# Moving two convolution taps to the start of a period, one accumulator to another bank, and one batch of operand preparation ahead of its use

## The chip, the cores and the metric

The kernel runs on one core of one Trainium2 chip, as one program. The metric is the device time of one execution in microseconds. The time before is a median over 3 runs; the profile is one further execution, recorded by the hardware profiler. The engines are named as the profile names them: PE is TensorE (PEld is its weight load), DVE is VectorE, ACT is ScalarE, POOL is GpSimd, SP is SyncE.

## What is computed

The input is a batch of two images of 128 channels and 64x64 pixels. Four layers follow each other:

```python
x = _L0_conv_ref(...)  # embedding, 2 x (Mamba scan + feed-forward), output projection, residual
x = _L1_conv_ref(...)  # q, k, v by 3x3 convolutions; softmax(q k^T / sqrt(c)) v over 4096 pixels; 1x1 conv; residual
x = _L2_conv_ref(...)  # q, k, v by 1x1 projections; softmax(q k^T) v over 4096 pixels; residual times gamma
x = _L3_conv_ref(...)  # attention over four scales at every pixel
```

The change touches layer 1 (its values) and layer 3. Layer 3, cut to what matters:

```python
for i, scale in enumerate((1, 2, 4, 8)):
    f = conv3x3(mean over scale x scale of x, conv_w[i], conv_b[i])   # scale 1: conv3x3 of x itself
    feats.append(bilinear_resize(f, h, w))
xr = stacked -> (b*h*w, 4, c)
q, k, v = split(xr @ attn_in_w.T + attn_in_b)        # 8 heads of 16 channels
attn = softmax(einsum('nhqd,nhkd->nhqk', q, k) / 4)  # 4 x 4 weights for each pixel and head
res = attn_out(einsum('nhqk,nhkd->nhqd', attn, v)) + xr
normed = layernorm(res)
out = einsum('bchw,oc->bohw', fused 4*c channels of normed, fus_w) + fus_b
```

## The kernel before

All data is fp32, with channels on the 128 partitions. Each layer is a block under a manual schedule: every engine executes its instructions in the order in which the code names them, and semaphores join the engines.

**Layers 1 and 2** are one loop over score units `now`, 128 units for each of four runs: runs 0 and 1 are layer 1 for image 0 and 1, runs 2 and 3 are layer 2. A unit is 128 query pixels by 1024 keys: `score` issues two matmuls (line 709) into a two-bank tile `pq`, and DVE copies it to SBUF with a running maximum (line 714). Later units follow with exponentials on ACT, 128x2048 transposes on DVE (`turn`, line 739), and from unit 14 (`LAG`) on the product with the values (line 759). At unit 13 of each run `values(r)` makes the value tensor. In layer 1 that is a 3x3 convolution in a transformed form: `inputs(r, cc)` makes, in twelve DVE operations of 128x288 elements (lines 589 to 600), six operand planes of a quarter of the image (four in `dlo`, two in a tile `dhi`), `products` multiplies them (line 612, tiles `pa` and `pb`), and `outputs` recombines them (lines 621 to 629). `chunks` walks over the four quarters and prepares the inputs of the next one while PE is at work on this one; the inputs of the first quarter are prepared at the start of `values`.

**Layer 3** works on 16 items (image, strip of 512 pixels). It is a software pipeline: `period(n)` runs for n from -2 to 16, and handles four items at different stages: r = n+2 (convolution at scale 1, features, q and first two k projections), m = n+1 (products of q and k, scores, softmax, v projections), p = n (weights times values, output projection, statistics) and o = n-1 (normalisation, fusion, store). The order inside a period is written by hand. PSUM has four pools here: `mm`, three one-bank tiles for projections, convolution, `po` and so far the fused output `pfus`; `pac`, one bank (tag "acc"), used by the scores `psc` and by the variances `pva` in turn; and `pwp`, one four-bank tile for the weights `pw` and the normalisation factors `prs`. A tile that asks for a bank waits until the last reader of the tile in it is done.

Names used below: conv tap matmul, line 1005, tile `pf`; projections, line 1032, tile `pqkv`; `product`, DVE, line 1049, tile `prod`; `scores`, line 1056; `weights`, line 1091; `weighted`, DVE, line 1098, tile `ov`; sums of `ov` by `add_ov`, line 1102; `soft_exp`, ACT, line 1074; `soft_sum`, DVE, lines 1080 to 1084; `mix_out`, lines 1111 to 1114; `newton`, lines 1133 to 1135; `factors`, line 1142; `normalise`, DVE, line 1149, tile `cen`; `fuse`, lines 1156 and 1161. Once per image change, `means`, `coarse_conv` (line 963, tile `pcs`) and `columns` for the second image are inserted into periods 2 to 5.

Of the kernel before, what the change touches and what calls it, by code (L numbers as in the profile page):

```python
# [6 lines left out]
F32 = mybir.dt.float32  # L7
# [8 lines left out]
P = 128  # L16
CH = 512
# [12 lines left out]
NS = len(SCALES)  # L30
# [37 lines left out]
def tile_conv_seq(ctx: ExitStack, tc, x, consts, vecs, wemb, wlay, wconv, wdt, wqkv, wsmall, wms, out):  # L68
# [478 lines left out]
    with ExitStack() as s, tc.manual_schedule():  # L547
# [29 lines left out]
        def inputs(r, cc):  # L577

            dhi = st["dhi"] = sp.tile([P, 2, 18, 16], F32, name="dhi", tag="d")
            d = [dlo[:, k] for k in range(4)] + [dhi[:, k] for k in range(2)]  # L580
            b = runs[r][1]

            def x1(k):

                return xt[:, b, 16 * cc : 16 * cc + 18, k : k + W - 3 : 4]

            tt, stt = nc.vector.tensor_tensor, nc.vector.scalar_tensor_tensor
            return [
                lambda: stt(d[0], x1(1), -4.0, x1(3), ALU.mult, ALU.add),
                lambda: stt(d[1], x1(2), -4.0, x1(4), ALU.mult, ALU.add),  # L590
                lambda: tt(d[0], d[1], d[0], ALU.subtract),
                lambda: stt(d[1], d[1], 2.0, d[0], ALU.mult, ALU.subtract),
                lambda: tt(d[2], x1(3), x1(1), ALU.subtract),
                lambda: tt(d[3], x1(4), x1(2), ALU.subtract),
                lambda: stt(d[2], d[2], -2.0, d[3], ALU.mult, ALU.add),
                lambda: stt(d[3], d[3], 2.0, d[2], ALU.mult, ALU.subtract),
                lambda: stt(d[4], x1(2), -5.0, x1(4), ALU.mult, ALU.add),
                lambda: stt(d[4], x1(0), 4.0, d[4], ALU.mult, ALU.add),
                lambda: stt(d[5], x1(3), -5.0, x1(5), ALU.mult, ALU.add),
                lambda: stt(d[5], x1(1), 4.0, d[5], ALU.mult, ALU.add),  # L600
            ]
# [58 lines left out]
        def values(r):  # L660
            vt = st["vt"] = sp.tile([P, N // P, C], F32, name="vt", tag="vt")
            vs = {}

            def turned(cc):
                for i in range(2):
                    pt = psa.tile([P, 4, P], F32, name="pvt", tag="acc")
                    for a in range(4):
                        at = (4 * i + a) * P
                        nc.tensor.transpose(pt[:, a, :], vs[cc][:, at : at + P], ident)
                    at = (2 * cc + i) * 4  # L670
                    nc.scalar.copy(vt[:, at : at + 4, :], pt)

            def to(cc):
                if cc > 1:
                    turned(cc - 2)
                vs[cc] = sp.tile([P, 4 * QG], F32, name="vs", tag="tr", bufs=2)
                return vs[cc]

            if not runs[r][0]:
                for f in inputs(r, 0):  # L680
                    f()
            chunks(r, 2, to)
            turned(NCC - 2)
            turned(NCC - 1)
# [126 lines left out]
        for now in range(NALL + LAG + 10):  # L811
            r, u = divmod(now, NU)
            w = now % 8
            if now < NALL:
                if u == 0:
                    if r == 2:
                        wm = wbig.tile([P, NS, 9, C], F32, name="wm", tag="wbig")
                        nc.sync.dma_start(wm, wms)
                    keys(r)
                    if runs[r][0]:  # L820
                        query(r, 0)

                r4, cc = divmod((now + 16) // 32, NCC)
                v = (now + 16) % 32
                if now >= 16 and r4 < B:
                    if v == 0:
                        ahead = inputs(r4, cc)
                    if v < 6:
                        for f in ahead[2 * v : 2 * v + 2]:
                            f()  # L830
                    if v == 14:
                        queries(r4, cc)
                        if r4 and cc == 0:
                            load(1, HI)
                score(r, u)
                if runs[r][0]:
                    if w == 2 and u // 8 + 1 < NU // 8:
                        query(r, u // 8 + 1)
                elif u == 1:
                    load(2, LO), load(2, HI)  # L840
                elif u == LAG:
                    load(0, LO), load(0, HI)
                    if r == 0:
                        load(1, LO)
            if w == 7:
                at(lambda r, u: finish_mm(r, u // 8), LAG + 9)
            at(product, LAG)
            if w == 7:
                at(lambda r, u: finish(r, u // 8), LAG + 9)
            if w in (3, 7):  # L850
                at(lambda r, u: exponentials(r, u // 4), 3)
            if w in (1, 5):
                at(lambda r, u: turn(r, u // 4, 0), 5)
            if w in (3, 7):
                at(lambda r, u: turn(r, u // 4, 1), 7)
            if w == 2:
                at(lambda r, u: diagonals(r, u // 8), 10)
            if w == 3:
                at(lambda r, u: spread(r, u // 8), 11)
            if w == 5:  # L860
                at(lambda r, u: divide(r, u // 8), LAG + 7)
            if now < NALL and u == LAG - 1:
                values(r)


    with ExitStack() as s, tc.manual_schedule():
# [130 lines left out]

        def conv(i, taps):
            b, c = items[i]
            if taps[0] == 0:  # L1000
                st[i]["pf"] = mmt("pf")
            for tap in taps:
                dy, dx = divmod(tap, 3)
                rhs = xt[:, b, c * RPC + dy : (c + 1) * RPC + dy, dx : dx + W]
                nc.tensor.matmul(st[i]["pf"], lhsT=wm[:, 0, tap, :], rhs=rhs, start=(tap == 0), stop=(tap == 8))  # L1005
# [145 lines left out]
        def fuse(i, sis):  # L1151
            w = st[i]
            if sis[0] == 0:
                w["pfus"] = mmt("pfus")
            for si in sis:
                nc.tensor.matmul(w["pfus"], lhsT=wfus[:, si, :], rhs=w["cen"][:, si, :], start=(si == 0), stop=(si == NS - 1))
            if sis[-1] < NS - 1:
                return
            b, c = items[i]
            ot = sp.tile([P, CH], F32, name="ot", tag="ot")  # L1160
            nc.scalar.activation(ot, w["pfus"], AF.Identity, bias=bfus)
            nc.sync.dma_start(out[b, :, c * RPC : (c + 1) * RPC, :].rearrange("c h w -> c (h w)"), ot)
            w.clear()

        def period(n, extra):
            o, p, m, r = n - 1, n, n + 1, n + 2

            def do(i, f, *a):
                if has(i):
                    f(i, *a)  # L1170

            def more(k):
                for f, a in extra.get((n, k), ()):
                    f(*a)


            do(r, features)
            do(m, project, 2, 0)
            for ti in range(NS):
                do(m, product, ti)  # L1180
                if ti == 0:
                    do(o, normalise)
                do(p, weights, ti)
                if ti + 2 < NS:
                    do(m, project, 1, ti + 2)
                if ti > 0:
                    do(m, scores, ti - 1)
                do(p, weighted, ti)
                if ti == 1 and has(p):
                    add_ov(nc.gpsimd, p, 0, 1)  # L1190
                if ti < 2:
                    do(o, fuse, (2 * ti, 2 * ti + 1))
                else:
                    do(r, conv, (2 * ti - 4, 2 * ti - 3))
                more(ti)
            do(m, scores, NS - 1)

            if has(p):
                add_ov(nc.vector, p, 2, 3)
                add_ov(nc.vector, p, 0, 2)  # L1200
            do(m, soft_max)
            do(r, conv, (4, 5, 6, 7, 8))
            do(r, conv_out)
            for si in range(1, NS):
                do(m, project, 2, si)
            do(m, soft_exp)
            do(m, soft_sum)
            more(4)
            for si in range(NS):
                do(p, mix_out, si)  # L1210
            more(5)

            do(p, variance)
            for si in range(NS):
                if si == 2:
                    do(p, newton)
                do(r, project, 0, si)
            do(r, project, 1, 0)
            do(p, factors)
            do(r, project, 1, 1)  # L1220
            more(6)
# [97 lines left out]
```

## Time and profile before

| | |
|---|---|
| time, median of 3 | 5120.4 us (5120.3 to 5123.17) |
| span of the profiled run | 5118.0 us |
| PE busy | 4685.8 us (92%) |
| DVE busy | 4091.4 us (80%) |
| ACT busy / POOL busy | 2366.8 us (46%) / 2312.5 us (45%) |
| mean granted PE clock | 0.947 of full speed |

Layer 0 fills about the first 42% of the span; layers 1 and 2 run from about 2160 us to 4295 us; layer 3 runs from about 4295 us to the end. A matmul of 128x512 fp32 stands as two records; back to back they start 0.43 us apart, so one such matmul takes 0.86 us of PE. "Idle before" in square brackets is the time that the engine stood still ahead of a row, with the instruction that released it.

### The profile page before, as it was taken

To read this page: it belongs to the slowest core of one execution; us is meant where nothing else is said; L and a number is where in the kernel's file an instruction comes from. 1 tells how busy PE (TensorE), PEld (TensorE's weight loads), DVE (VectorE), ACT (ScalarE), POOL (GpSimd) and SP (SyncE) were. 2 spreads that over 40 slices of the span, in tenths; PEclk is the share of its full clock that TensorE was granted. 3 is DMA by queue.
4 is the path that set the end of the run, shared out by engine and by line. 5 is a ranking of instruction groups with operands and counts; after the bars stand their busy time and mean duration, and the time that the engine had idled before them with its cause. 6 is when DMAs were issued, how large, how long until landed. Compare 5 with 4: busy or idle time off the path is not lost.

```text
span 5118.0 us, 48991 instructions
## 1 busy us (share of the span) xinstructions
PE 4685.8 (92%) x14797; PEld 2250.5 (44%) x14797; DVE 4091.4 (80%) x4416; ACT 2366.8 (46%) x3221; POOL 2312.5 (45%) x1948
## 2 busy tenths in 40 slices
PE   5898899899888998789999999999999998989997
PEld 1222222222222222356666666666666665333332
DVE  5999999999999999588888887667766775757665
ACT  4677777777777777422322222333333332223332
POOL 2777777766777777313332233333333333323221
PEclk8889998998999989899999999999999999999998
DMA  5332323333222333124443244444444442000000
GB/s 151 72 69 69 69 69 71 71 71 69 67 67 67 69 72 72 38 56 104 100 105 86 71 103 105 118 98 111 112 100 98 111 112 62 5 5 7 5 7 9
DMA packets 237017, 373.86 MB, mean 73 GB/s; under 512 B 88001, under 2 KB 88401, under 8 KB 228433
## 3 DMA queue, kind: packets, MB, share of 16 engines
q1 hardware_dynamic: 187600, 303.55, 25.0%
q10 hardware_dynamic: 49152, 67.17, 5.5%
q8 instruction: 118, 1.93, 0.2%
q14 instruction: 147, 1.20, 0.1%
HBM read 92.18 MB, written 9.83 MB: 20 GB/s over the span
## 4 chain that ended last, share of the span: by engine, by line
PE 47%; POOL 19%; DVE 13%; issue 10%; DMA 4%; ACT 3%; SPq 2%; ACTq 0%; DVEq 0%; POOLq 0%
POOL h L387 15%; PE po L759 13%; PE pq L709 13%; DVE tr L739 3%; PE pf L1005 3%; DMA pt<-tr 2%; PE py L399 2%; SPq L750 2%; PE pqkv L1032 1%; PE pu L288 1%; DVE prod L1049 1%; DVE h L384 1%; PE psc L1056 1%; PE pw L1091 1%; POOL dtu L347 1%
## 5 line engine op out<-in xcount | busy, mean ns | idle before, releaser
L746 POOL COPY pt<-tr 32x512 f32<-32x512 f32 x1024 | 652.3, 637 | 1499.3 <-DVE tr L739 766.6
L384 DVE TENSOR_TENSOR_SCAN h<-da,carry,h 128x512 f32<-128x512 f32 x1024 | 1240.7, 1265 | 60.6 <-ACT da L373 30.6
L387 POOL TENSOR_TENSOR h<-h,cb 128x2048 f32<-128x2048 f32 x256 | 1161.2, 4536 | 20.8 <-POOL carry L386 0.2
L709 PE MATMUL pq<-k,q 128*128 128x512 f32 x2048 | 963.9, 594 | 8.5 <-DVE sc L714 6.2
L759 PE MATMUL po<-pt,vt 128*128 128x256 f32 x4096 | 967.3, 379 | 2.4 <-DMA pt<-tr 2.4
L724 ACT ACTIVATE sc<-sc,nm 128x2048 f32<-128x2048 f32 x256 | 510.6, 1995 | 925.4 <-DVE nm L720 670.8
L714 DVE TENSOR_SCALAR_CACHE_REDUCE sc<-pq 128x1024 f32<-128x1024 f32 x512 | 624.8, 1222 | 362.1 <-PE pq L709 340.5
L759 PEld LDWEIGHTS po<-pt,vt 128*128 128x128 f32 x4096 | 779.1, 190 | 295.2 <-issue 211.4
L373 ACT ACTIVATE da<-dtb,am 128x512 f32<-128x512 f32 x1024 | 681.6, 684 | 223.8 <-DVE h L384 212.5
L739 DVE STREAM_TRANSPOSE tr<-sc 128x2048 f32<-128x2048 f32 x256 | 591.7, 2311 | 68.1 <-DMA pt<-tr 61.2
L366 DVE TENSOR_TENSOR h<-bb,pdu 128x2048 f32<-128x2048 f32 x256 | 581.3, 2271 | 77.3 <-PE py L399 29.4
L399 PE MATMUL py<-h,sel 128*32 128x512 f32 x2048 | 511.1, 643 | 1.6 <-POOL h L387 1.6
L709 PEld LDWEIGHTS pq<-k,q 128*128 128x128 f32 x2048 | 383.6, 190 | 286.6 <-issue 247.7
L360 PE MATMUL pdu<-dtu,fsel 128*128 128x512 f32 x512 | 327.3, 725 | 102.5 <-DVE h L366 102.4
L399 PEld LDWEIGHTS py<-h,sel 128*32 128x32 f32 x2048 | 115.3, 118 | 416.3 <-issue 409.4
L288 PE MATMUL pu<-xn,wu 128*128 128x512 f32 x512 | 245.3, 612 | 3.8 <-ACT xn L278 2.0
L360 PEld LDWEIGHTS pdu<-dtu,fsel 128*128 128x128 f32 x512 | 96.3, 215 | 309.7 <-DVE h L366 187.7
L386 POOL COPY carry<-h 128x4 f32<-128x4 f32 x256 | 47.5, 186 | 388.9 <-DVE h L384 388.9
L1032 PE MATMUL pqkv<-f,ws 128*128 128x512 f32 x384 | 189.9, 620 | 11.5 <-DVE prod L1049 9.9
L1098 DVE TENSOR_TENSOR ov<-v,pw 128x2048 f32<-128x2048 f32 x64 | 146.0, 2282 | 50.6 <-PE pw L1091 50.3
L1102 POOL TENSOR_TENSOR ov<-ov 128x2048 f32<-128x2048 f32 x16 | 72.6, 4540 | 240.8 <-DVE ov L1098 240.8
L1016 POOL TENSOR_SCALAR f<-lo 128x256 f32<-128x256 f32 x32 | 27.6, 863 | 315.1 <-PE po L1111 260.5
(241 smaller groups left out, 5387.1 us busy)
## 6 DMA issues: line engine op xcount, KB each, us to landing
pt<-tr SPq DMA_DIRECT2D x2048, 64.0 KB, 2.0
dtb<-dt SPq DMA_DIRECT2D x1024, 64.0 KB, 2.0
pt<-tr ACTq DMA_DIRECT2D x1024, 64.0 KB, 2.2
bb<-dr SPq DMA_DIRECT2D x128, 256.0 KB, 4.7
cb<-dr SPq DMA_DIRECT2D x128, 256.0 KB, 7.7
uw<-ufold SPq DMA_DIRECT2D x14, 576.0 KB, 3.9
xt<-in_x SPq DMA_DIRECT2D x16, 256.0 KB, 5.1
xr<-in_x SPq DMA_DIRECT2D x16, 256.0 KB, 2.9
```

The costliest lines, as they stand in the source:

```text
L360: nc.tensor.matmul(pdu, lhsT=four(s_ % 4), rhs=st[i]["dtu"][:, s_ // 4, :], start=True, stop=True)
L366: nc.vector.tensor_tensor(h, st[i]["bc", 0], pdu.unsqueeze(1).to_broadcast([P, 4, CH]), ALU.mult)
L373: nc.scalar.activation(da, st[i]["dtb", s_], AF.Exp, scale=am[items[i][1]][:, j, gg, m : m + 1])
L384: nc.vector.tensor_tensor_scan(h[:, m, :], da, h[:, m, :], carries[b, l][:, j, gg, m : m + 1], ALU.mult, ALU.add)
L387: nc.gpsimd.tensor_tensor(h, h, st[i]["bc", 1], ALU.mult)
L399: nc.tensor.matmul(py[r : r + 32, :], lhsT=sel, rhs=st[i]["h", s_ + k][:, m, :], start=(m == 0), stop=(m == 3), tile_position=(0, r),)
L709: nc.tensor.matmul(pq[:, i, :], lhsT=st["q", r, grp][:, it * P : (it + 1) * P], rhs=st["k"][:, at : at + CH], start=True, stop=True)
L714: nc.vector.tensor_scalar(dst, pq, 1.0, None, ALU.mult, ALU.max, accum_out=st["mx"][:, c2 : c2 + 1])
L724: nc.scalar.activation(sc, sc, AF.Exp, bias=nm, scale=scale, accum_out=sm[:, hh : hh + 1])
L739: nc.vector.transpose(tr, st.pop(("sc", r, blk, hh)).rearrange("p (t r f) -> p r t f", r=NB, f=32))
L746: nc.gpsimd.tensor_copy(dst, src)
L759: nc.tensor.matmul(st["po", r, grp], lhsT=st["vt"][:, jt, :], rhs=rhs, start=(jt == 0), stop=(jt == N // P - 1))
```

## The change

Three things are changed.

1. In `values`, the twelve `inputs` of the first quarter are no longer made at the start of `values` (unit 13), but two at a time in units 6 to 11, behind the score copy of each unit.
2. In layer 3, the fused output `pfus` takes the one-bank pool `pac` instead of a tile of `mm`, and its four matmuls all stand at step 0 of the period, where they had been split into two at step 0 and two at step 1.
3. In layer 3, the first two taps of item r's convolution are issued at the start of the period, where item m's first v projection had been; the next taps stand at steps 1, 2 and 3, and one tap remains behind the scores. The v projection joins the other three behind the convolution.

The purpose is to give PE work where it waits for DVE at the start of the period and at its second step, and to take DVE work off the start of `values`. The matmuls, vector operations and bytes are the same in number as before.

```diff
@@ values
-            if not runs[r][0]:
-                for f in inputs(r, 0):
-                    f()
             chunks(r, 2, to)
@@ main loop of layers 1 and 2
                 elif u == 1:
                     load(2, LO), load(2, HI)
+                    first = inputs(r, 0)
+                elif 6 <= u < 12:
+                    for f in first[2 * u - 12 : 2 * u - 10]:
+                        f()
@@ fuse
-                w["pfus"] = mmt("pfus")
+                w["pfus"] = pac.tile([P, CH], F32, name="pfus", tag="acc")
@@ period
             do(r, features)
-            do(m, project, 2, 0)
+            do(r, conv, (0, 1))
...
-                if ti < 2:
-                    do(o, fuse, (2 * ti, 2 * ti + 1))
-                else:
-                    do(r, conv, (2 * ti - 4, 2 * ti - 3))
+                if ti == 0:
+                    do(o, fuse, range(NS))
+                do(r, conv, ((), (2, 3), (4, 5), (6, 7))[ti])
                 more(ti)
             do(m, scores, NS - 1)
...
-            do(r, conv, (4, 5, 6, 7, 8))
+            do(r, conv, (8,))
             do(r, conv_out)
-            for si in range(1, NS):
+            for si in range(NS):
                 do(m, project, 2, si)
```

More of the change, by code (lines that the diff above doesn't have):

```diff
@@ L999, in conv @@
             b, c = items[i]
+            if not taps:
+                return
             if taps[0] == 0:
```

## The prediction

> **What bounds the kernel now.** I read the page first: PE is busy 92% and DVE 80%, and the chain of waits puts 47% of the span on PE and 13% on DVE. That is a mean over four layers, so I went to the two places that the diff touches, with the timeline of PE, then of DVE and ACT, over one ordinary period of layer 3 and over both calls of `values`.
>
> One ordinary period of layer 3, from `weights` to `weights`, PE alone. The columns are start, busy time, engine, line; the bracket is idle time ahead of the row:
>
> ```profile
> 4717.63 1.14 PE L1091 MATMUL pw<-at,spread 32*128 32x512 f32 x8 [1.89 <-DVE cen L1149]
> 4718.70 1.13 PE L1032 MATMUL pqkv<-f,ws 128*128 128x512 f32 x2
> 4719.66 1.88 PE L1156 MATMUL pfus<-cen,wfus 128*128 128x512 f32 x4
> 4721.48 1.14 PE L1091 MATMUL pw<-at,spread 32*128 32x512 f32 x8
> 4723.44 1.13 PE L1032 MATMUL pqkv<-f,ws 128*128 128x512 f32 x2 [0.83 <-DVE prod L1049]
> 4724.50 1.07 PE L1056 MATMUL psc<-prod,kc 128*32 128x512 f32 x8
> 4725.50 1.98 PE L1156 MATMUL pfus<-cen,wfus 128*128 128x512 f32 x4
> ...
> 4736.37 4.56 PE L1005 MATMUL pf<-xt,wm 128*128 128x512 f32 x10
> 4740.77 2.74 PE L1032 MATMUL pqkv<-f,ws 128*128 128x512 f32 x6
> 4743.34 1.02 PE L1111 MATMUL po<-f,kc 128*128 128x512 f32 x2
> ...
> 4761.79 1.14 PE L1091 MATMUL pw<-at,spread 32*128 32x512 f32 x8 [1.89 <-DVE cen L1149]
> ```
>
> The period is 4761.79 - 4717.63 = 44.16 us, and PE stands still visibly in two places: 1.89 us, until `normalise` has freed the four-bank tile, and 0.83 us, until `product` 1 has freed the bank that the last k projection takes. Everything else is PE work. The same two waits stand in nearly every period from 1 to 14.
>
> What DVE does there:
>
> ```profile
> 4721.05 2.34 DVE L1049 SCALAR_TENSOR_TENSOR prod<-pqkv,vec,q 128x2048 f32<-128x2048 f32 x1
> 4723.31 2.27 DVE L1098 TENSOR_TENSOR ov<-v,pw 128x2048 f32<-128x2048 f32 x1
> 4725.50 2.34 DVE L1049 SCALAR_TENSOR_TENSOR prod<-pqkv,vec,q 128x2048 f32<-128x2048 f32 x1
> 4728.62 2.29 DVE L1098 TENSOR_TENSOR ov<-v,pw 128x2048 f32<-128x2048 f32 x1 [0.78 <-PE pw L1091]
> ```
>
> Products and weighted values alternate, 2.3 us each, almost without a gap: DVE is close behind PE here.
>
> In `values` of run 1, PE and then DVE:
>
> ```profile
> 2813.93 1.89 PE L759 MATMUL po<-pt,vt 128*128 128x256 f32 x8
> 2821.37 7.89 PE L612 MATMUL pa<-uw 128*128 128x256 f32 x24 [5.54 <-DVE uw L591]
> 2831.68 5.34 PE L612 MATMUL pa<-uw 128*128 128x256 f32 x24
> ```
> ```profile
> 2792.59 1.23 DVE L714 TENSOR_SCALAR_CACHE_REDUCE sc<-pq 128x1024 f32<-128x1024 f32 x1 [1.38 <-PE pq L709]
> 2814.13 1.23 DVE L714 TENSOR_SCALAR_CACHE_REDUCE sc<-pq 128x1024 f32<-128x1024 f32 x1 [1.80 <-PE pq L709]
> 2818.42 1.01 DVE L589 SCALAR_TENSOR_TENSOR uw<-xt 128x288 f32<-128x288 f32 x1
> 2826.65 0.67 DVE L589 SCALAR_TENSOR_TENSOR uw<-xt 128x288 f32<-128x288 f32 x1
> ```
>
> PE waits 5.54 us for the first inputs and then runs its first 24 records in 7.89 us instead of 5.34. The first set of inputs occupies DVE from 2818.42 to 2826.65, 8.2 us. From there to the end of `values` DVE has no gap above 0.3 us: `values` is bound by DVE.
>
> [...] a `pf` that lives from the start of the period to its end leaves two `mm` banks; this is why `pfus` must move. The trace shows no bank but the waits for them (0.83 us above). [...] after 1.89 us a `weights` group takes 1.14 us, after 6.48 us idle (4668.16) a `factors` group takes 2.09 instead of 1.14. [...] an input operation takes 1.08 us beside POOL's copies of transposed blocks and 0.67 without.
>
> **Layer 3, one period.** I lay out the new order from `weights` 0 as time 0, with group times from the rows above (start to start: `weights` 1.07, projection 0.96, scores 1.0, two taps 1.91, fusion matmul 0.86).
> - Start: two taps (1.71 us) replace one projection (0.86). They stand in the 1.89 us wait, which shrinks to 1.03; time 0 does not move, since `cen` sets it through q, `prod`, `prs` on DVE, none of it changed. 0.86 us of PE work is hidden.
> - Step 0: projection k2 at 1.07, four fusion matmuls 2.03 to 5.5, so `weights` 1 at 5.55 instead of 3.85. The k3 projection comes at 6.6; `product` 1 ends at 5.76 (4723.39 - 4717.63), so the 0.83 us wait is gone.
> - New wait 1: `scores` 0 at 7.65 needs the bank that `pfus` holds. Its eviction (0.69 us) is next in ACT's queue and ends at 6.4. No stall; queued behind it on PE are the taps.
> - New wait 2: `weights` 1 comes later, so `weighted` 1 starts at 6.75 instead of 5.68. DVE then stands at 11.3 after `product` 2; `weights` 2 ends at 11.65, `weighted` 2 11.8 to 14.05, `weights` 3 at 14.5 finds it done; DVE ends the sums of `ov` at 23.2 instead of 22.4. PE reaches `po` at 23.9 instead of 25.71, and the half that needs `ov` at 24.8: 1.6 us to spare.
> - ACT: four v evictions end at 24.9; `soft_exp` waits for DVE until 25.4 and ends at 26.0, as the first `po` becomes readable (25.8). At most 0.2 us.
>
> From time 0 to `po` the period so gains 25.71 - 23.9 = 1.8 us, and the rest is unchanged: 42.4 us instead of 44.16.
>
> **Other periods.** Ordinary in this sense are 1, 3, 4 and 6 to 13, 11 periods: 19.7 us. In 3 and 4 a `coarse_conv` at step 1 finds all three banks taken and waits for `product` 2, until about 11.4 with PE there at 10.6; in its place stood 0.87 and 0.78 us of waiting for the eviction, so it is even. In period 2 (`means`) and 5 (`columns`) DVE is the bound behind `soft_sum`, which comes 1.05 us earlier (`soft_exp` ends at 26.0 against 27.1): 1.05 us gained in 2; in 5 the following start has no wait to hide taps in (`weights` at 4673.47 shows none, and PE is at half speed after 6.48 us idle), which costs 1.6 us: net -0.5. Period 0 is bound by DVE in its steps, the taps fill waits of 1.26 and 0.40 us: about +2. Period -1: -0.2. Drain: in 14 there is no convolution left, DVE's later `weighted` costs 0.4; in 15 two more fusion matmuls stand ahead of `weights` 1, for which DVE already waits: 1.8 lost. Sum 19.7 + 1.05 - 0.5 + 2 - 0.2 - 0.4 - 1.8 = 19.9 us. The unknown is DVE's shift: if the 0.8 us on DVE reaches PE the period gains 1.0, if the hidden small waits of PE go too, 2.1: 11 to 24 us.
>
> **Values.** Run 1: PE is busy without a gap in units 6 to 13, DVE has idle time there of 1.38 + 0.25 + 1.33 + 0.24 + 0.72 + 0.25 + 1.80 + 0.24 = 6.2 us. Twelve operations (8.2 us at the price beside POOL, 7.4 at that without) fill it, some 1.5 us spill over. PE is not held up: the score of unit 13 at 2812.22 needs the copy of unit 11, done by 2810.8 even so. PE starts `pa` at 2815.9 at once, and DVE's second set starts at 2820.1 instead of 2826.65: 6.5 us. Behind the two inputs on DVE wait the copies and transposes of the unit; their users come several units later. Run 0: no products exist yet, DVE is the bound already in units 6 to 13, with idle time of about 1 us (0.24 + 0.25 + 0.28 + 0.24), so the 6.53 us PE wait at the start of `values` moves rather than disappears: 1 us. Ends: 4 (idle time only half usable) and 9.5. I take 7.5.
>
> Total 19.9 + 7.5 = 27.4 us: 5093.
>
> **Rivals.**
> - DVE takes over in layer 3: the 1.07 us that `weighted` 1 loses is passed on to `po` or to the next start. For it: DVE is busy 31 of 44 us and its operations stand end to end in the steps. Against: 1.6 us of slack at `po`, idle of 6.35 us ahead of `newton`. Layer 3 then gains about 0.86 x 12 = 10: 5120 - 10 - 7.5 = 5103.
> - The values' inputs gain nothing (they only move DVE work): 5120 - 20 = 5100. For it: run 0. Against: the 6.2 us of idle DVE in run 1.
> - The shared bank becomes the new wait: variances, fused output and scores now run in series through one bank. If the eviction came 3 us late, as behind a blocked ACT, PE would lose 1.8 us net in 12 periods, more than the two waits bring: layer 3 loses 2 us or more beyond its gain, and with values' inputs delaying scores the time would be 5130. Against: ACT is idle 11.05 us ahead of that eviction now.
>
> **Chances.** The forecast 0.62, first rival 0.17, second 0.09, more gain than forecast (hidden waits) 0.07, slower or equal 0.05. The range takes the forecast with the ends of its terms and the first two rivals: 5085 to 5104. Faster by over 0.2% (under 5110) 0.93, same 0.04, slower 0.03.
>
> **What would show it.** Right: periods of about 42.4 us between evictions of `pfus`; the wait for `cen` near 1.0 and that for `prod` gone; no wait of `psc` for the eviction; `pa` of run 1 without wait and 5.3 us long; in run 0 the scores of units 6 to 13 stretched by some 7 us. Wrong: PE waiting for `ov` at `po`, or for the bank at `psc`, or scores of run 1 waiting for DVE in units 8 to 13.

## The result, and the profile after

| | before | after |
|---|---|---|
| time, median of 4 runs each | 5121.65 us (5120.3 to 5123.17) | 5102.76 us (5101.34 to 5104.57) |
| ratio | | 0.9963, 95% interval 0.9946 to 0.998 |
| PE busy in the profiled run | 4685.8 us | 4686.2 us |
| DVE busy in the profiled run | 4091.4 us | 4094.2 us |

The changed kernel is faster by 18.9 us; 27.4 were forecast. Five more runs on another occasion gave 5102.3 us, ratio 0.9963 again (0.9949 to 0.9976). The busy times are as before: what went is waiting. The two executions that were profiled took 5118.0 and 5102.8 us, a difference of 15.2 us; whatever is read from the two traces has to add up to that and not to 18.9.

One ordinary period of layer 3 after the change, the timeline of PE from `weights` to `weights` (columns as before: start, busy time, engine, line; idle time in brackets; line numbers are 3 higher than before):

```profile
4755.46 1.14 PE L1094 MATMUL pw<-at,spread 32*128 32x512 f32 x8 [1.03 <-DVE cen L1152]
4756.53 1.12 PE L1035 MATMUL pqkv<-f,ws 128*128 128x512 f32 x2
4757.50 3.60 PE L1159 MATMUL pfus<-cen,wfus 128*128 128x512 f32 x8
4761.02 1.14 PE L1094 MATMUL pw<-at,spread 32*128 32x512 f32 x8
4762.10 1.13 PE L1035 MATMUL pqkv<-f,ws 128*128 128x512 f32 x2
4763.15 1.06 PE L1059 MATMUL psc<-prod,kc 128*32 128x512 f32 x8
4764.15 1.98 PE L1008 MATMUL pf<-xt,wm 128*128 128x512 f32 x4
...
4775.02 1.13 PE L1008 MATMUL pf<-xt,wm 128*128 128x512 f32 x2
4775.98 3.60 PE L1035 MATMUL pqkv<-f,ws 128*128 128x512 f32 x8
4779.42 1.02 PE L1114 MATMUL po<-f,kc 128*128 128x512 f32 x2
...
4797.87 1.14 PE L1094 MATMUL pw<-at,spread 32*128 32x512 f32 x8 [1.03 <-DVE cen L1152]
```

The period is 4797.87 - 4755.46 = 42.41 us. The wait for `cen` is 1.03 us, the wait for `product` 1 is gone, `po` comes 23.96 us behind `weights` and does not wait for `ov`, and the scores do not wait for the bank.

DVE in the same period:

```profile
4758.88 2.34 DVE L1052 SCALAR_TENSOR_TENSOR prod<-pqkv,vec,q 128x2048 f32<-128x2048 f32 x1
4762.23 2.29 DVE L1101 TENSOR_TENSOR ov<-v,pw 128x2048 f32<-128x2048 f32 x1 [1.01 <-PE pw L1094]
4764.44 2.35 DVE L1052 SCALAR_TENSOR_TENSOR prod<-pqkv,vec,q 128x2048 f32<-128x2048 f32 x1
4767.27 2.29 DVE L1101 TENSOR_TENSOR ov<-v,pw 128x2048 f32<-128x2048 f32 x1 [0.49 <-PE pw L1094]
```

The new wait on DVE is there, 1.01 us ahead of `weighted` 1, and nobody on PE waits for it.

`values` of run 1, PE and then DVE:

```profile
2809.22 1.89 PE L756 MATMUL po<-pt,vt 128*128 128x256 f32 x8
2812.09 0.71 PE L767 MATMUL pr<-dg,kc 128*128 128x128 f32 x4 [0.98 <-DVE dg L761]
2819.53 5.34 PE L612 MATMUL pa<-uw 128*128 128x256 f32 x24
2827.30 5.34 PE L612 MATMUL pa<-uw 128*128 128x256 f32 x24
```
```profile
2793.74 0.68 DVE L589 SCALAR_TENSOR_TENSOR uw<-xt 128x288 f32<-128x288 f32 x1
2794.34 1.12 DVE L590 SCALAR_TENSOR_TENSOR uw<-xt 128x288 f32<-128x288 f32 x1
2823.04 1.04 DVE L589 SCALAR_TENSOR_TENSOR uw<-xt 128x288 f32<-128x288 f32 x1
2824.01 1.11 DVE L590 SCALAR_TENSOR_TENSOR uw<-xt 128x288 f32<-128x288 f32 x1
```

The 5.54 us of waiting ahead of `pa` are gone and `pa` takes 5.34 us. A new wait of 0.98 us stands ahead of `pr`, whose operand `dg` is now queued behind two input operations on DVE.

To see where time went between such places, I followed a mark that comes once per eight score units, the `pr` matmuls of layers 1 and 2, through both traces. The table says how much later (+) or earlier (-) the changed kernel is than the kernel before at each mark, in us; below this is called its lateness:

```
group of run 0, before / behind its values    +7.34 / +0.92   (+0.59 at the end of layer 0)
all further groups of run 0                   +0.93 to +0.96
run 1, before / behind its values             +2.62, +3.76 / -2.26
all further groups of run 1                   -2.22 to -2.26
run 2, before / behind its values             -2.25 / -0.83
run 3, before / behind its values             +0.34 / +2.84, then constant
first coarse convolution of layer 3           +0.92
end                                           -15.2
```

Between starts of runs and their values the difference stands still to 0.05 us. Run 1's values gain 2.62 + 2.26 = 4.9 us. The jumps of +1.7 (start of run 1), +1.4, +1.2 and +2.5 us, and one of -1.9 us between the end of run 3 and layer 3, stand at places that the change does not touch. Together they are +4.9 us: in these two traces they take back all that run 1's values gain.

### The profile page after: what moved, and what is told of

It is laid out like the page before. It is cut to its first block, busy times and chain, and to the rows that moved or that the text cites. A ratio compares the mean times of both kernels' runs of the same rounds, so it can differ in the third digit from the quotient of the medians.

```text
span 5102.8 us, 48990 instructions
## 1 busy us (share of the span) xinstructions
PE 4686.2 (92%) x14797; PEld 2249.2 (44%) x14797; DVE 4094.2 (80%) x4416; ACT 2367.7 (46%) x3221; POOL 2317.8 (45%) x1948
## 4 chain that ended last, share of the span: by engine, by line
PE 46%; POOL 21%; DVE 13%; issue 11%; DMA 4%; ACT 3%; SPq 3%; DVEq 0%; ACTq 0%; POOLq 0%
POOL h L387 17%; PE po L756 13%; PE pq L706 13%; DVE tr L736 3%; DMA pt<-tr 2%; SPq L747 2%; PE pf L1008 2%; PE py L399 2%; PE pqkv L1035 2%; PE pw L1094 1%; POOL dtu L347 1%; POOL z L410 1%; PE pfus L1159 1%; PE pu L288 1%; PE psc L1059 1%
## 5 line engine op out<-in xcount | busy, mean ns | idle before, releaser
L261 PE MATMUL pr<-rs,kc 2*128 2x512 f32 (+1 forms) x128 | 90.2, 834 | 77.3 <-POOL rs L257 71.1
```

## Experiments

Five questions: what each part is worth alone, whether the jumps belong to the change, which edit in layer 3 does it, what start and drain cost, and whether a better order exists. Times are medians, ratios are against the kernel before on the same chip. The experiments ran on three chips, so those of different groups are best compared by what each gains on the kernel before.

**Inputs alone.** Part 1 of the diff on the kernel before.

> Only the first inputs of the values are made ahead; layer 3 is as before. My theory: run 1 gains 4 to 5 us at its values, run 0 nothing, since DVE is the bound there already; then 5117, with up to 3 us more or less from untouched places where PE's clock falls in gaps of about 3 us. Rival (the inputs only move DVE work): 5121.

5115.75 us against 5120.18, ratio 0.9992 (0.9984 to 1.0001). In the marks, run 0 loses 0.1 to 0.3 us at its values (+0.14 here, +0.33 and +0.31 in the two traces of the changed kernel), run 1 gains 4.85. This is the size expected, 4.4 us by the medians, but its interval just touches no change.

**Layer 3 alone.** Parts 2 and 3.

> Only layer 3 is changed (fusion in one block in the other bank, two taps at the start); values as before. My theory: periods of 42.4 us, layer 3 shorter by 15 to 18 us: 5104, give or take 3. Rival (the two parts only pay together): 5110 or more.

5101.63 us, ratio 0.9966 (0.9954 to 0.9977); ordinary periods 42.40 us. Layer 3 is nearly the whole gain. 4.4 + 18.6 is 23.0, while the whole kernel gains 19 on both occasions: see the last experiment.

**The fusion block alone.**

```diff
-                if ti < 2:
-                    do(o, fuse, (2 * ti, 2 * ti + 1))
-                else:
+                if ti == 0:
+                    do(o, fuse, range(NS))      # pfus in pac
+                if ti > 1:
                     do(r, conv, (2 * ti - 4, 2 * ti - 3))
```

> Only the fused output is moved to the scores' bank with its four matmuls at step 0; the taps stay at steps 2 and 3 and behind the scores, the v projection at the start. My theory: the wait for the k bank (0.83 us) goes, but PE has nothing at step 1 to cover the weighted value that comes 1 us later, so waits of some 0.4 us before weights 2 and 0.6 us before weights 3 take its place: period 44.0 to 44.4, time 5121 to 5123. Rival (the fusion block is what gains): period 43.3, time 5111.

5120.48 us, ratio 1.0 (0.9991 to 1.0008). The timeline of PE over one period of it (44 us), the rows of `weights`:

```profile
4724.20 1.14 PE L1091 MATMUL pw<-at,spread 32*128 32x512 f32 x8
4727.75 1.14 PE L1091 MATMUL pw<-at,spread 32*128 32x512 f32 x8 [0.36 <-DVE ov L1098]
4732.21 1.14 PE L1091 MATMUL pw<-at,spread 32*128 32x512 f32 x8 [0.41 <-DVE ov L1098]
4762.61 1.14 PE L1091 MATMUL pw<-at,spread 32*128 32x512 f32 x8 [1.89 <-DVE cen L1149]
```

The wait of 0.83 us is traded for two of 0.36 and 0.41 us: most ordinary periods are 43.97 us instead of 44.16, two of the eight from 6 to 13 are 45.62. What is left of this gain goes in the drain, the last periods: from `weights` of period 14 to the start of the last fusion it takes 84.1 us, where the kernel before takes 79.4. So the block in itself brings nothing; it needs PE work at step 1, and the loss in the drain is its own.

**A later start, nothing else.** In the kernel before, the first of the twelve input operations at the very start of layer 1 is made three times.

```diff
-        for f in inputs(0, 0):
+        head = inputs(0, 0)
+        for f in 2 * head[:1] + head:
             f()
```

> The kernel before, with the first input operation of layer 1 made three times instead of once, so that all of layers 1 to 3 starts 1.3 us later; nothing else differs. My theory (PE's clock falls or not in the 3 us gaps at the starts of runs and in their values[...]): the lateness against before does not stay at 1.3 us, it jumps by 1 to 3 us, up or down, at the keys and values of runs 1, 2 and 3, and is constant between. Rival (the jumps of the changed kernel come from its own changes): 1.3 us throughout, up to the end.

The one execution took 5121.37 us. The added operations did not do what they were meant to do. PE's first products of layer 1 wait for a DMA and not for these operations, and are not held up by the added ones. The kernel before, then this one:

```profile
2155.59 7.98 PE L612 MATMUL pa<-uw 128*128 128x256 f32 x24 [3.77 <-DMA uw<-ufold]
```
```profile
2157.03 8.05 PE L612 MATMUL pa<-uw 128*128 128x256 f32 x24 [3.63 <-DMA uw<-ufold]
```

PE starts 1.44 us later, but at the end of layer 0, ahead of the added operations, it was already 1.6 us late: this lateness is a difference between two executions of the same instructions. What the run still shows is how it goes on: +0.73 in the rest of run 0, +0.72 in run 1, then -0.97 at the start of run 2, +0.43 behind its values, +1.48 from run 3 on. Places that no edit touches moved by -1.7, +1.4 and +1.05 us, and the times between them by nothing. The two traces of the changed kernel itself say the same: the second is 0.8 us earlier than the first all through runs 0 to 2, and 3.3 us earlier from run 3's values on. So jumps of this kind need no change of the kernel. What they are shows in run 3's values, where PE waits equally long in both kernels. Before the change, then after it:

```profile
3851.75 1.09 PE L669 MATMUL pvt<-kc,vs 128*128 128x128 f32 x8 [3.16 <-ACT vs L561]
```
```profile
3852.09 1.97 PE L669 MATMUL pvt<-kc,vs 128*128 128x128 f32 x8 [3.16 <-ACT vs L561]
```

The same eight transposes behind the same wait of 3.16 us take 1.09 us in one trace and 1.97 in the other. The clock granted to PE from 3851 to 3853 us was full in the first (1.00) and half in the second (0.50). In the second trace of the changed kernel they take 1.09 us again. The jump at the start of run 1 is of the same kind: behind a wait of 2.32 us in both traces a `pb` group takes 2.86 us before and 4.39 after, and the granted clock stays at 1.00 in the first (2763.4 to 2766.2 us) and falls to 0.50 in the second (2766.0 to 2768.0 us). The same wait has either outcome, even in two executions of one kernel; what decides between them is not seen in the traces.

**Without taps at the start.** The changed kernel, with the v projection back at the start and the taps one step later.

```diff
-            do(r, conv, (0, 1))
+            do(m, project, 2, 0)
-                do(r, conv, ((), (2, 3), (4, 5), (6, 7))[ti])
+                do(r, conv, ((), (0, 1), (2, 3), (4, 5))[ti])
-            do(r, conv, (8,))
+            do(r, conv, (6, 7, 8))
```

> The changed kernel, but with the v projection at the start of the period as before, and the taps at steps 1, 2 and 3 with three left behind the scores. My theory (the block of fusions removes the k wait if taps cover step 1; the taps at the start are worth 0.86 us a period by themselves): period 43.3, wait for cen 1.89, time about 11 us above the changed kernel. Rival (the taps at the start are what removes both waits): period 44.0 as with the fusion block alone, 20 us above.

5123.19 us, ratio 1.0002 (0.9993 to 1.001): 21 us above the changed kernel, the rival's number, but not for the rival's reason. Its ordinary periods are 43.26 us, as I expected, or 44.91 us, in the order of two long ones to one short one. A short one and a long one, PE from `weights` 0 to `weights` 1:

```profile
4804.11 1.14 PE L1094 MATMUL pw<-at,spread 32*128 32x512 f32 x8 [1.89 <-DVE cen L1152]
4805.18 1.12 PE L1035 MATMUL pqkv<-f,ws 128*128 128x512 f32 x2
4806.14 3.60 PE L1159 MATMUL pfus<-cen,wfus 128*128 128x512 f32 x8
4809.67 1.14 PE L1094 MATMUL pw<-at,spread 32*128 32x512 f32 x8
...
4847.37 1.23 PE L1094 MATMUL pw<-at,spread 32*128 32x512 f32 x8 [1.89 <-DVE cen L1152]
4848.53 2.08 PE L1035 MATMUL pqkv<-f,ws 128*128 128x512 f32 x2
4850.40 4.25 PE L1159 MATMUL pfus<-cen,wfus 128*128 128x512 f32 x8
4854.58 1.14 PE L1094 MATMUL pw<-at,spread 32*128 32x512 f32 x8
```

`weights` 0 to `weights` 1 takes 5.56 us in the first and 7.21 in the second; the projection takes 2.08 us instead of 1.12. The wait of 1.89 us ahead of both is the same. The granted clock is 0.78 on the mean from 4847.2 to 4855.0 us in the long one and 1.00 from 4803.9 to 4808.0 us in the short one. The kernel before had this too, in two of its ordinary periods (44.99 and 44.97 us instead of 44.16); the prediction took no notice of them.

**The wait filled with useless work.** As the last, with one matmul more per period that nobody reads (periods 1 to 13).

```diff
             do(m, project, 2, 0)
+            if has(o) and has(r):
+                wrm = pac.tile([P, CH], F32, name="wrm", tag="acc")
+                nc.tensor.matmul(wrm, lhsT=ident, rhs=kc[:, :CH], start=True, stop=True)
```

> As the kernel without taps at the start (periods of 43.26 and 44.91 us), with one useless 128x512 matmul of 0.86 us in the wait for cen, into the scores' bank, read by nobody. My theory (the 1.89 us wait costs more than itself where PE's clock falls behind it; a wait of 1.03 us does not let it fall): all ordinary periods 43.3, although PE does 0.86 us more each; time about 5111 to 5113, some 10 us below the kernel without taps at the start. Rival (the long periods come from DVE or from banks): 43.26 and 44.91 as without the matmul, 5121 to 5123.

5109.48 us, ratio 0.9979 (0.9971 to 0.9988). PE at one of its periods:

```profile
4837.21 1.02 PE L1184 MATMUL wrm<-kc 128*128 128x512 f32 x2
4839.27 1.14 PE L1094 MATMUL pw<-at,spread 32*128 32x512 f32 x8 [1.03 <-DVE cen L1152]
4840.34 1.12 PE L1035 MATMUL pqkv<-f,ws 128*128 128x512 f32 x2
```

Every period from 6 to 12 is 43.26 or 43.27 us; no long one is left. The next is 44.91 us again: it ends behind the start of period 14, which has no such matmul. Against the kernel before on its own chip this one gains 9.9 us, where the kernel without the added matmul loses 1.5: one matmul per period without a reader makes the kernel some 11 us faster. So the wait of 1.89 us cost more than its length, and the taps at the start are worth their 0.86 us and the clock.

**Taps and the v projection in the wait.**

```diff
+                if ti == 0:
+                    do(m, project, 2, 0)
                 do(p, weights, ti)
...
-            for si in range(NS):
+            for si in range(1, NS):
                 do(m, project, 2, si)
```

> The changed kernel, with the first v projection behind the two taps but still ahead of weights 0, so that both stand in the wait for cen. My theory (the wait of 1.03 us takes another 0.86, DVE still has time to spare at po): period 41.6, 10 us below the changed kernel. Rival (DVE becomes the bound at po): period 42.0 to 42.4 with a wait of po for ov.

5096.15 us, ratio 0.9948 (0.9935 to 0.9962). Ordinary periods are 41.55 us, with 0.17 us of waiting for `cen` and none at `po`. It is 6 us below the changed kernel and not 10: its drain, from `weights` of period 14 to the start of the last fusion, takes 85.8 us against 83.9 there, and the periods 2 and 5, with `means` and `columns` in them, are no shorter than there.

**Start and drain in another order.** As the last, but periods without an item o or r keep the old order, with taps at steps 1 to 3; `pfus` is in `mm` again in periods 14 to 16, where no `pf` exists.

```diff
+            full = has(o) and has(r)
+            if full:
                 do(r, conv, (0, 1))
+            else:
+                do(m, project, 2, 0)
...
+                if not full and ti < 2:
+                    do(o, fuse, (2 * ti, 2 * ti + 1))
```

> As the one with taps and v in the wait, but periods -2 to 0 and 14 to 16, where item o or item r does not exist, have the v projection at the start, fusions in two halves in a bank of mm, and taps at steps 1 to 3. My theory (the start and the drain lost what I had not counted: the k3 projection waiting for product 1 in periods -1 and 0 since pf holds one of three banks, and four fusion matmuls ahead of weights 1 in the drain): 4 to 6 us below the one with taps and v. Rival [...]: within 2 us of it.

5085.71 us, ratio 0.9933 (0.9919 to 0.9946): 10.4 us below the last one, more than expected, and the best of the orders tried without useless work. From the first coarse convolution to `weights` of period 1 it takes 103.7 us instead of 107.6, and 80.0 us instead of 85.8 in the drain.

**PE kept busy in layer 2.** As the last, with six useless matmuls (2.6 us) ahead of the third chunk of keys and values in runs 2 and 3.

> As the kernel with its ends repaired, with six useless matmuls (2.6 us) in the keys and in the values of runs 2 and 3, where PE stands still some 3 us for ACT; read by nobody. My theory (the clock falls in these gaps or not [...], the jumps of 1 to 3 us at these places): no half-speed rows behind the gaps, the lateness against before no longer grows at keys and values of runs 2 and 3, 2 to 4 us below the one with its ends repaired. Rival (the useless matmuls stand in the way of what waits for them): no gain, or up to 4 us lost.

5084.46 us, ratio 0.993 (0.9914 to 0.9947), 1.3 us below the last one but on another chip; against their own kernels before the two gain 34.9 and 36.0 us, so nothing is shown of a gain. In the one trace the lateness falls by 1.7 us at the start of run 2 and of run 3 each, where the changed kernel had risen by 1.2 us at run 3, it no longer rises at either run's values, and the transposes of run 3's values take 1.09 us behind a wait of 0.60 us. That is what the theory expects, but one trace does not show it: without useless matmuls the kernel with the later start also fell by 1.7 us at run 2, and the one without taps at the start does not rise at either run's values.

**The changed kernel again.**

> The changed kernel once more, since each part alone summed to more (4.4 and 18.6 us by medians) than the whole gained in its first four runs (18.9). If the parts add up: 5097. If the whole loses in its own way[...]: 5102 to 5103 again.

5102.3 us over 5 runs, so the parts do not add up, by some 4 us, which the interval of the inputs alone would just allow. The marks of this trace have jumps of +1.7, +1.4 and +1.2 us at starts and values of runs 1 to 3. Such jumps come without any edit of those places, as the two experiments with a later start and with the fusion block alone show too; in the traces before and after the change the granted clock differs at each of the three (1.00 and 0.64, 1.00 and 0.54, 0.69 and 0.55). But the first of them, at the start of run 1, stands in all eight traces of kernels with the inputs made ahead, measured against the one trace of the kernel before, and in one of the three others, the fusion block alone. That would make some of the missing time a cost of making the inputs ahead; with one trace each, whether it does stays open.

## Why the forecast was right in direction and too large

The time of 5102.76 us lies inside the range of 5085 to 5104, but by 1.2 us only, and at the number that the first rival named (5103), though that rival's mechanism is absent from the rows. The mechanism forecast for the ordinary period is in the rows; that the errors in the other terms left the total just inside the range is luck.

Held, with what was measured: the ordinary period (42.4 forecast, 42.41); the wait for `cen` (1.03) and that for `product` 1 (gone); no wait of the scores for the shared bank, no wait at `po`; `means` (1.05 forecast, 0.94 gained); coarse convolutions even (0.80 us of waiting in each of the two, where 0.87 and 0.78 had been); the stretched scores of run 0 (some 7 us forecast, 6.75). `columns` held in the first trace of the changed kernel (-0.5 forecast, -0.56), but in its second trace the same period is 1.6 us shorter. The first rival (DVE takes over) and the third (the shared bank) fell by the same rows. The second (the inputs gain nothing) held for run 0 and failed for run 1.

Four terms of the sum were mis-sized.

1. Start, periods -1 and 0: +1.8 us forecast, -2.0 measured (from the first coarse convolution to `weights` of period 1, 105.7 us before and 107.7 after). The waits in period 0 that the taps were to fill did go, but one new wait came in each of the two periods. I counted the `mm` banks for an ordinary period, where the fusion block covers the time until `product` 1, but not for periods without an item o. `pf` holds one bank from the start on, so the last k projection has to wait there, and in period 0 the clock fell behind the wait (0.55 granted from 4379.8 to 4381.9 us, where period -1 has 1.00 from 4351.9 to 4353.1). The timeline of PE after the change:

```profile
4351.92 1.13 PE L1035 MATMUL pqkv<-f,ws 128*128 128x512 f32 x2 [1.13 <-DVE prod L1052]
4379.88 1.97 PE L1035 MATMUL pqkv<-f,ws 128*128 128x512 f32 x2 [1.12 <-DVE prod L1052]
```

2. Drain: -2.2 us forecast, -4.5 measured to the start of the last fusion (79.4 us before, 83.9 after), -3.2 to its end, since that fusion takes 6.41 us before and 5.18 after. The cause was right, and the fusion block alone shows the same loss; its price was taken at full clock. In period 15, at a granted clock of 0.74 (5053.3 to 5058.3 us), the block takes

```profile
5053.32 4.94 PE L1159 MATMUL pfus<-cen,wfus 128*128 128x512 f32 x8
5058.20 1.14 PE L1094 MATMUL pw<-at,spread 32*128 32x512 f32 x8
```

where four matmuls take 3.60 us otherwise (at 1.00 from 4755.4 to 4759.0 us), and DVE waits for `weights` 1 behind it; `weights` 3 of the same period takes 2.09 us instead of 1.14 (0.50 granted from 5065.3 to 5067.5 us). The order with repaired ends, which undoes 1 and 2 on top of the taps and the v projection, returned 3.9 and 5.8 us there.

3. Values: 7.5 us forecast, about 4.5 measured (run 1 4.9 of 6.5, run 0 -0.3 of 1). In run 1 the work did go into DVE's idle time, and DVE's second set of inputs, which now comes first in `values`, starts 6.2 us earlier than it had if the lateness of 2.6 us is taken off (2823.04 against 2826.65). But this set is now as dear as the first had been, beside POOL's copies (its first two operations take 1.04 and 1.11 us in place of 0.67, rows above), which costs 1.4 us. The prediction's price, dear beside POOL's copies and cheap without, is too simple: three of the moved operations are dear too (1.12, 1.10 and 0.89 us), but others with POOL busy for nearly all of their time take 0.67 and 0.68 us. In run 0 nothing was to be had, as DVE was the bound.

4. The clock, which I had priced only behind long waits. The prediction read one `weights` group of 1.14 us behind a wait of 1.89 us as a sign that such a wait costs no clock. The same trace had this one:

```profile
4805.95 1.99 PE L1091 MATMUL pw<-at,spread 32*128 32x512 f32 x8 [1.89 <-DVE cen L1149]
```

The granted clock is 0.53 from 4805.9 to 4809.0 us, and 1.00 from 4717.6 to 4721.0 us behind the same wait. The clock gave 1.65 us back in layer 3 (two long periods before, none after among the ordinary ones) and took 4.9 us in all at the untouched places: the clock granted there before and after the change is 1.00 and 0.64 at the start of run 1, 1.00 and 0.54 at run 2's values, 0.69 and 0.55 at the start of run 3, 1.00 and 0.50 at its values, and 0.89 and 1.00 at its end.

For the two profiled executions the sum closes: 27.4 - 3.8 (start) - 1.0 (drain, to its end) - 3.0 (values) + 1.65 - 4.9 (clock) - 0.5 (the rest of the periods 1 to 13) - 0.6 (lateness that came from layer 0) = 15.3 us, against 15.2 measured. The medians differ by 18.9 us; how much of the jumps stands in the executions without a profile is not known.

## What to carry to other kernels

Price a wait of TensorE with the clock behind it: here a wait of 1.89 us cost up to 1.65 us more than its length, and filling part of it paid, with needed work and even with useless work (some 11 us for one matmul per period). When a tile's life is lengthened in a pool, count the pool's banks in the first and last rounds of the pipeline too, where other tiles that covered the wait are missing. Follow a periodic mark through both traces: where the difference stands still nothing changed. Before a jump is credited to an edit, or called the clock, compare two traces of one kernel and the granted clock at that place.

## What the runs showed of the hardware

Behind a wait of only 1.89 us in a 43 us period PE's clock fell in two of three periods, at 1.65 us each, in the kernel without taps at the start (granted 0.78 from 4847.2 to 4855.0 us behind such a wait, 1.00 from 4803.9 to 4808.0 us in a short period). In the kernel before it fell to 0.50 behind the same wait (4806.3 to 4807.3 us). Where the wait was filled to 1.03 us, the clock fell behind it in none of the ordinary periods (`weights` 0 takes 1.14 us in all of them). How often it falls differs between kernels with the same wait: two of three periods at 43.26 us; at 44.16 us two of the eight that have nothing inserted before the drain, at 0.8 us each; at 43.97 us two of eight, at 1.65 us. Waits of 2.32 and 3.16 us had either outcome (1.00 and 0.50 granted behind each). What decides between the outcomes was not shown.
